# One launch with two transformer layers: score matmuls over 64 features, row differences and rotary partners by on-chip transfers, weights fetched one head group ahead

## The chip, the core and the metric

The kernel runs on one core of a Trainium2 chip. The core has five engines that matter here: TensorE (PE in the profile, with its weight loads as PEld), VectorE (DVE), ScalarE (ACT), GpSimd (POOL) and SyncE (SP), which issues nearly all transfers. Each engine runs its own instructions in the order in which they were written; between engines there are semaphores. The metric is the device time of one launch in microseconds, lower is better.

## What is computed

The input is `x`, 16 batches of 256 tokens with 256 features, and a second array of the same shape. Two layers follow, each of the form x = x + attention(condition(x)) and x = x + ffn(condition(x)). All numbers are fp32. The part that the change concerns is the second layer's attention:

```python
# condition: a reaction-diffusion step on the 256 x 256 array of one batch
lap_x = y[:, s, d-1] - 2 y[:, s, d] + y[:, s, d+1]      # reflected at the edges
lap_y = y[:, s-1, d] - 2 y[:, s, d] + y[:, s+1, d]      # reflected at the edges
u = zX * lap_x + zY * lap_y + zR * y * (1 - y)
# attention: 16 heads of 64 features, segments of 128 tokens, 16 memory keys and values per head
z = u * rsqrt(mean(u * u) + eps) * g
q, k, v = split(z @ W_qkv)
q, k = rotary(q), rotary(k)        # pairs of features (even, odd) are turned by an angle
scores = q @ concat(memory_k, k).T / 8     # inside a segment, causal
x = x + softmax(scores) @ concat(memory_v, v) @ W_out
```

Before it come a cross attention, a 16-head causal attention with 16 features a head and a feed-forward net on numbers quantized in blocks of 16. After it comes a mixture of experts: 8 experts, of which each token uses 2, and a shared one.

## The kernel before

**Two parts.** `woven` does everything up to the second attention, batch by batch; `mixture` does the rest. The change touches only `woven`, and `setup`, where an array in DRAM is made.

**Streams and the planner.** In `woven` each stage is a generator that yields single operations: `stage_a` and `stage_e` (cross attention and first attention), `stage_gate`, `stage_up`, `stage_down` (quantized weights, once), `stage_f` (first feed-forward net), `stage_p` (diffusion and projections), `stage_g` (scores and softmax), `stage_v` (values, output projection, store of the batch). `weave` keeps one waiting operation of each stream, estimates when it could start, and writes the earliest one next; ties go to the stream that stands earlier in the list. The estimate has a cost per operation, 0.15 us for a hop between engines (`HOP`), and 4.5 us from a transfer's issue until its data are there (`LANDING`). What it writes is a fixed order for every engine. Counters in `g.done` keep the stages apart: a group of four heads may be projected when fewer than three groups are ahead of the values; the diffusion of a batch begins when its feed-forward net is done.

**Diffusion** (`diffuse`). `y` is a batch as [128 partitions, 2, 256]: token s lies in partition s mod 128, half s div 128. The difference along the features is made by POOL from shifted slices. The difference along the tokens crosses partitions, and is a product with a constant 256 x 256 matrix `lap`: four matmuls into PSUM (`ply`), which DVE multiplies by `zy` and adds to `u`.

**Projection** (`project4`), for each of four groups of four heads, in each of 16 batches. The group's weights are loaded at its start: `wq` (two transfers), `wv`, `wo`. The columns of `w_qk1` come from the host ordered so that a 256-column block holds four heads' even features in its first 128 columns and the odd ones in the last. So PE leaves in `pq[:, 0, :]` the even features of four heads, 32 partitions each, and in `pq[:, 1, :]` the odd ones, for the same partitions. DVE multiplies by cosine into `f_t1` and by sine into `f_t2`; POOL makes two combinations of 128x256 each for the queries (`f_q`) and two for the keys (`keys0` to `keys3`, one tile per group, kept).

**Scores** (`scores4`). A head's 64 features lie in two pieces of 32 partitions. Each of two segments and four heads is therefore two matmuls of 32 rows by 144 columns that add up in PSUM: 16 a group, in two steps of two heads. DVE adds the mask and takes the maximum, ACT exponentiates, POOL scales.

**Order on the queues.** SP has the loads, the zero-writes of `ysort` (two of 1 MB a batch, in `stage_f`), the stores of a batch (`xd`) and all that the change adds. POOL has the joins, the first attention's triangular masks (`b_e`), the softmax scalings (`f_prob`, `f_pm`) and half of the quantization.

The names of the steps to follow: in `diffuse` (line 860) `lap`, `lx`, `u`; in `project4` (line 897) `wq`, `f_t1`, `f_t2`; in `scores4` (line 955) the innermost loop; in `project_heads` (line 467) `b_t1`, `b_t2`; in `weave` (line 182) the rule in `ready`.

Of the kernel before, what the change touches and what calls it, by code (L numbers as in the profile page):

```python
# [19 lines left out]
P = 128  # L20
S = 256
# [41 lines left out]
def setup(ctx, tc, a, n_batch):  # L63
# [28 lines left out]
    k.zero = c.tile([P, D], F32, name="zero")  # L92
    nc.gpsimd.memset(k.zero, 0.0)

    k.xd = [dram.tile([S, D], F32, name=f"xd{b}") for b in range(n_batch)]
# [86 lines left out]
def weave(streams):  # L182
# [8 lines left out]
    def ready(op, engine):  # L191
        t = 0.0
        for n in names(op.ins):
            when, by = written.get(n, (0.0, engine))
            t = max(t, when + (HOP if by != engine else 0.0))
        for x in op.outs:
            n = x.tensor.name
            before = [written.get(n), read.get(n)]
            ring = rings.get(getattr(x.tensor, "tag", None), [])
            if n not in ring and ring:  # L200
                bufs = x.tensor.bufs or x.tensor.tag_meta.bufs
                if len(ring) >= bufs:
                    before += [written.get(ring[-bufs]), read.get(ring[-bufs])]
            for p in before:
                if p:
                    t = max(t, p[0] + (HOP if p[1] != engine else 0.0))
        return t
# [84 lines left out]
def woven(k):  # L292
    nc, tc = k.nc, k.tc
    with ExitStack() as ctx:
# [12 lines left out]
        g.live, g.kT = {}, {}  # L307
        g.x, g.io, g.done = {}, {}, {"W": 0, "A": 0, "M": 0, "E": 0, "F": 0, "P": 0, "G": 0, "V": 0, "L": 0}
        with tc.manual_schedule():
            weave([stage_a(g), stage_e(g), stage_gate(g), stage_up(g), stage_down(g), stage_f(g), stage_p(g), stage_g(g), stage_v(g)])  # L310

# [101 lines left out]
def fetch_a(g, b):  # L413

    a = g.a
    g.x[b] = g.xp.tile([P, 2, D], F32, name="x", tag="x")
    xT = g.a_.tile([P, 2, S], F32, name="xT", tag="xT", bufs=2)
    fT = g.a_.tile([P, 2, S], F32, name="fT", tag="fT")
# [48 lines left out]
def project_heads(g, hT):  # L467
# [8 lines left out]
    for st in range(2):  # L476
# [11 lines left out]
        table = lambda t: t[:, st, :].unsqueeze(1).to_broadcast([P, 2 * H, DH0 // 2])  # L488
        t1, t2 = tile_a(g, 2 * D, "b_t1"), tile_a(g, 2 * D, "b_t2")
        for r in range(2):  # L490
            yield g.dve.tensor_tensor(pairs(t1)[:, :, :, r], pairs(qk)[:, :, :, r], table(g.cos0), ALU.mult)
            sin = table(g.sin0 if r else g.nsin0)
            yield g.dve.tensor_tensor(pairs(t2)[:, :, :, r], pairs(qk)[:, :, :, 1 - r], sin, ALU.mult)
        for i, dst in enumerate((qp, kp)):
            half = slice(i * D, (i + 1) * D)
            yield g.pool.tensor_tensor(dst[:, st, :, 0:DH0], by_head(t1[:, half]), by_head(t2[:, half]), ALU.add)

# [298 lines left out]


def stage_p(g):
    k, a = g.k, g.a
    yield lambda: g.done["A"] > 0 and g.done["W"] == 3  # L800
    g.lap, op = load(g, g.w, "lap", [P, 2, S], a["lap"])
    yield op
    g.z = []
# [34 lines left out]

    g.keys = []
    for n in range(4):  # L840
        pmk = tile_l(g, [P, 2, 4 * PM], "pmk", 2)
        yield g.sp.dma_start(out=pmk, in_=a["pmk"][:, n])
        t = g.w.tile([P, 2, 2, PM + P], F32, name=f"keys{n}")
        for j in range(4):
            rows = row32(j, 32)
            src = pmk[rows, :, j * PM : (j + 1) * PM]
            yield g.pool.tensor_copy(t[rows, :, :, 0:PM], src.unsqueeze(2).to_broadcast([32, 2, 2, PM]))
        g.keys.append(t)
    g.mhalf = g.w.tile([P, 2], F32, name="mhalf")
    yield g.pool.memset(g.mhalf, -0.5)  # L850
    for b in range(g.B):
# [44 lines left out]

def project4(g, n, zT):

    a = g.a
    wq = tile_l(g, [P, 2, 2, 2 * P], "wq", 2)  # L900
    for which in range(2):
        cols = slice((8 * which + 2 * n) * P, (8 * which + 2 * n + 2) * P)
        yield g.sp.dma_start(out=wq[:, which], in_=a["w_qk1"][:, :, cols])
    wv, wo = tile_l(g, [P, 2, 4 * DH1], "wv", 2), tile_l(g, [P, 2, D], "wo", 3)
    yield g.sp.dma_start(out=wv, in_=a["w_v1"][:, :, n * 4 * DH1 : (n + 1) * 4 * DH1])
    yield g.sp.dma_start(out=wo, in_=a["w_out1"][:, 2 * n : 2 * n + 2, :])
    q = tile_l(g, [P, 2, S], "f_q", 3)
    by_seg = lambda t: t.rearrange("p (s t) -> p s t", s=2)
    for which in range(2):
        one = yield from single(g, wq, zT)  # L910
        pq = one.rearrange("p (r t) -> p r t", r=2)
        for r in range(2):
            yield from mm_(g, pq[:, r, :], [(wq[:, which, c, r * P : (r + 1) * P], zT[:, c, :]) for c in range(2)])
        t1, t2 = tile_l(g, [P, 2, S], "f_t1"), tile_l(g, [P, 2, S], "f_t2")
        cos, sin = (g.cos1, g.sin1) if which else (g.cosq, g.sinq)
        yield g.dve.tensor_tensor(t1, pq, cos.unsqueeze(1).to_broadcast([P, 2, S]), ALU.mult)
        yield g.dve.tensor_tensor(t2, pq, sin.unsqueeze(1).to_broadcast([P, 2, S]), ALU.mult)
        g.singles.append(one)
        dst = [g.keys[n][:, r, :, PM:] if which else by_seg(q[:, r, :]) for r in range(2)]
        yield g.pool.tensor_tensor(dst[0], by_seg(t1[:, 0, :]), by_seg(t2[:, 1, :]), ALU.subtract)  # L920
        yield g.pool.tensor_tensor(dst[1], by_seg(t1[:, 1, :]), by_seg(t2[:, 0, :]), ALU.add)
    v = tile_l(g, [P, 2, 4 * DH1], "f_v", 3)
# [5 lines left out]
    g.singles.append(one)  # L928
    return q, v, wo

# [23 lines left out]

def scores4(g, n, q, v, wo):

    keys = g.keys[n]
    prob = tile_l(g, [P, 2, 4, PM + P], "f_prob", 2)
    if n % 2 == 0:
# [550 lines left out]
```

## Time and profile before

| what | value |
|---|---|
| median of three runs | 2944.68 us (2943.74 to 2948.99) |
| profiled execution: its own time | 2943.53 us |
| profiled execution: span | 2941.8 us |
| mean granted TensorE clock | 0.963 |
| last matmul of `woven` ends | about 1896 us |
| DMA over the span | 265.66 MB, mean 90 GB/s |
| POOL: joins of `f_q` and of `keys` | 128 + 128, mean 734 and 762 ns |
| DVE: product with the `lap` result | 16, mean 751 ns |
| SP: one 128 KB or contiguous 256 KB load | about 0.33 to 0.47 us of issue |

A busy time is the time in which at least one instruction of that engine ran. A group row gives line, engine, operation, the tile written and those read, the shapes, the number of records, then busy time and mean duration of one, then the engine's idle time just before them and what ended it. Nearly all operations of the woven part pass through one helper and have its line, L160; they are told apart by tile names. Records of an fp32 matmul come in pairs.

### The profile page before, as it was taken

To read this page: it belongs to the slowest core of one execution; us is meant where nothing else is said; L and a number is where in the kernel's file an instruction comes from. 1 tells how busy PE (TensorE), PEld (TensorE's weight loads), DVE (VectorE), ACT (ScalarE), POOL (GpSimd) and SP (SyncE) were. 2 spreads that over 40 slices of the span, in tenths; PEclk is the share of its full clock that TensorE was granted. 3 is DMA by queue.
4 is the path that set the end of the run, shared out by engine and by line. 5 is a ranking of instruction groups with operands and counts; after the bars stand their busy time and mean duration, and the time that the engine had idled before them with its cause. 6 is when DMAs were issued, how large, how long until landed. Compare 5 with 4: busy or idle time off the path is not lost. (4 is left out here: it accounts for less than half of the span.)

```text
span 2941.8 us, 42036 instructions
## 1 busy us (share of the span) xinstructions
PE 2768.7 (94%) x15979; PEld 2072.5 (70%) x15979; DVE 1428.6 (49%) x3073; ACT 924.0 (31%) x2416; POOL 842.2 (29%) x1023
## 2 busy tenths in 40 slices
PE   5899999999999999999999989689999999999999
PEld 3666667777777777767777767545566888888865
DVE  6566666676676676675776655413240000000023
ACT  2223333333333333423334333223321222222221
POOL 4333333433344343343343333202220000000034
PEclk7799999999899999999999999889999999999999
DMA  3122122122122132222221222231111355555523
GB/s 107 55 93 73 53 92 84 56 80 74 59 91 69 58 97 69 63 92 69 64 92 35 76 90 74 87 93 51 51 38 67 108 179 179 179 181 179 177 85 95
DMA packets 191230, 265.66 MB, mean 90 GB/s; under 512 B 34217, under 2 KB 161970, under 8 KB 181682
## 3 DMA queue, kind: packets, MB, share of 16 engines
q1 hardware_dynamic: 184882, 246.16, 26.2%
q0 software_dynamic: 6144, 16.79, 1.8%
q8 instruction: 128, 2.10, 0.3%
q14 instruction: 76, 0.62, 0.1%
HBM read 202.34 MB, written 60.56 MB: 89 GB/s over the span
## 5 line engine op out<-in xcount | busy, mean ns | idle before, releaser
L160 ACT ACTIVATE f_prob<-pair,f_stat 128x144 f32<-128x144 f32 x512 | 190.7, 377 | 270.2 <-DVE f_stat L160 258.8
L160 DVE TENSOR_TENSOR pair<-pair,mask 128x256 f32<-128x256 f32 (+1 forms) x384 | 197.8, 516 | 123.1 <-PE pair L160 83.2
L49 PE MATMUL bank<-ysT,w 128*128 128x256 f32 x1120 | 249.3, 381 | 5.7 <-ACT ysT L113 5.7
L160 PE MATMUL single<-e_zT,wq 128*128 128x256 f32 x1024 | 254.1, 392 | 0.0
L1155 POOL DMA_INDIRECT got<-osort,pos_o x64 | 62.3, 973 | 662.8 <-ACT hT L1103 608.5
L49 PE MATMUL bank<-w,ehT 128*128 128x256 f32 x1120 | 247.4, 379 | 0.0
L49 PEld LDWEIGHTS bank<-ysT,w 128*128 128x128 f32 x1120 | 211.3, 190 | 38.0 <-ACT ysT L113 9.9
L49 PEld LDWEIGHTS bank<-w,ehT 128*128 128x128 f32 x1120 | 212.8, 190 | 28.9
L160 PEld LDWEIGHTS single<-e_zT,wq 128*128 128x128 f32 x1024 | 193.4, 196 | 32.9 <-issue 2.7
L1140 ACT ACTIVATE ehT<-bank,own_b 128x256 f32<-128x256 f32 x280 | 132.5, 473 | 241.6 <-PE bank L49 241.6
L160 POOL TENSOR_SCALAR_AFFINE_SELECT b_e<-b_e 128x512 f32<-128x512 f32 x128 | 86.5, 676 | 329.9 <-ACT b_e L160 329.9
L160 PE MATMUL pair<-keys,f_q 32*128 32x144 f32 x2048 | 164.9, 300 | 0.9 <-ACT b_e L160 0.7
L160 PEld LDWEIGHTS pair<-keys,f_q 32*128 32x128 f32 x2048 | 137.2, 190 | 35.9 <-issue 28.6
L160 ACT ACTIVATE b_e<-pair 128x768 f32<-128x768 f32 x128 | 103.6, 810 | 166.4 <-PE pair L160 153.3
L160 PE MATMUL single<-wo,f_oT 128*128 128x256 f32 x512 | 129.8, 386 | 9.5 <-ACT f_oT L160 8.4
L160 POOL TENSOR_TENSOR f_q<-f_t,f_t 128x256 f32<-128x256 f32 x128 | 91.6, 734 | 160.9 <-DVE f_t L160 151.4
L160 PE MATMUL pair<-b_qkT 16*128 16x128 f32 (+1 forms) x1024 | 127.3, 373 | 11.0 <-ACT b_qkT L160 8.0
L1145 DVE COPY eo<-bank 128x512 f32<-128x512 f32 x35 | 24.2, 692 | 230.9 <-PE bank L49 230.9
L160 DVE TENSOR_REDUCE qpad<-pair 128x2 f32<-128x256 f32 (+1 forms) x256 | 131.0, 554 | 4.4
L1259 POOL DMA_INDIRECT ysort<-r_y,r_posi x64 | 62.6, 978 | 241.0 <-DMA ysort<-r_y,r_posi 97.0
L160 DVE TENSOR_TENSOR x<-x,single 128x512 f32<-128x512 f32 (+1 forms) x112 | 68.0, 607 | 128.7 <-PE single L160 128.1
L160 POOL TENSOR_TENSOR keys<-f_t,f_t 128x256 f32<-128x256 f32 x128 | 95.2, 762 | 118.8 <-DVE f_t L160 117.6
(295 smaller groups left out, 5319.7 us busy)
## 6 DMA issues: line engine op xcount, KB each, us to landing
w<-in_w SPq DMA_DIRECT2D x70, 1024.0 KB
ysort<-zero SPq DMA_DIRECT2D x32, 1024.0 KB
wq<-in_w_qk SPq DMA_DIRECT2D x128, 256.0 KB
wv<-in_w_v SPq DMA_DIRECT2D x64, 256.0 KB
wo<-in_w_out SPq DMA_DIRECT2D x64, 256.0 KB
ys<-ysort SPq DMA_DIRECT2D x35, 256.0 KB
osort<-eo SPq DMA_DIRECT2D x35, 256.0 KB
xT<-in_xT SPq DMA_DIRECT2D x16, 256.0 KB
```

The lines of the kernel that those rows point to most:

```text
L49: nc.tensor.matmul(out, lhsT, rhs, start=start and i == 0, stop=stop and i == last)
L160: return Op([(self.name, self.cost(fn, outs, aps), lambda: call(*args, **kw))], outs, aps)
L1140: nc.scalar.activation(hT[:, f, :], ph, AF.Gelu_apprx_tanh, bias=b1[:, f : f + 1])
L1145: nc.vector.tensor_copy(o, po)
L1155: nc.gpsimd.indirect_dma_start(out=g, out_offset=None, in_=k.osort[:, :], in_offset=bass.IndirectOffsetOnAxis(ap=r.pos_o[:, i, t : t + 1], ...
L1259: nc.gpsimd.indirect_dma_start(out=k.ysort[:, :], out_offset=bass.IndirectOffsetOnAxis(ap=posi[:, i, t : t + 1], axis=0), in_=y, in_offset ...
```

## The change

It has these parts.

- **Scores over 64 features.** The columns of the query and key weights are put in another order: for each pair of heads the 32 even and then the 32 odd features of one head, then of the other. A head then lies in 64 neighbouring partitions, and a score is one matmul of 64 rows. The reordering is done once on the chip, by a new stage `stage_order`, which loads eight blocks, has POOL copy them in the new order and stores them in a DRAM array `wqk`. `stage_p` waits for it.
- **Rotary partners by transfer.** Even and odd features of a head are now in different partitions. After DVE's products, four transfers of 32 partitions each exchange neighbouring blocks of the sine product from `f_t2` into `f_t3`, and POOL adds `f_t1` and `f_t3` in one 128x512 operation. The sign is in the sine table. The addition for the queries is written after the keys' transfers, that for the keys after the value projection.
- **Second difference by neighbours' rows.** The four `lap` matmuls go. `up` and `down` are `y` moved by one partition, each a transfer of 127 partitions, with four transfers of one partition for the rows at the edges of the halves. POOL adds them, DVE subtracts twice `y` and adds the product with `zy`.
- **Weights a group ahead.** `fetch_p` loads `wq` and `wv` for the next group before the present one is projected; `wo` is loaded in `scores4`.
- **Order of streams and the planner.** `stage_g` stands ahead of `stage_p` in the list, `stage_order` before `stage_f`. In `ready`, an operation of SP no longer waits for an earlier SP operation on the same buffer.
- **Space.** `xT` has one buffer instead of two; in `project_heads` the cosine product is written in place and `b_t1` goes; `f_t1` and `f_t3` have two buffers, `f_t2` one.

```diff
-            yield g.dve.tensor_tensor(pairs(t1)[:, :, :, r], pairs(qk)[:, :, :, r], table(g.cos0), ALU.mult)
             sin = table(g.sin0 if r else g.nsin0)
             yield g.dve.tensor_tensor(pairs(t2)[:, :, :, r], pairs(qk)[:, :, :, 1 - r], sin, ALU.mult)
+        for r in range(2):
+            yield g.dve.tensor_tensor(pairs(qk)[:, :, :, r], pairs(qk)[:, :, :, r], table(g.cos0), ALU.mult)
...
+def stage_order(g):
+
+    k = g.k
+    for i in range(8):
+        cols = slice(i * 2 * P, (i + 1) * 2 * P)
+        raw, out = tile_l(g, [P, 2, S], "f_t1", 2), tile_l(g, [P, 2, S], "f_t3", 2)
+        yield g.sp.dma_start(out=raw, in_=g.a["w_qk1"][:, :, cols])
+        for c in range(2):
+            dst = out[:, c].rearrange("p (j r d) -> p j r d", j=4, r=2)
+            yield g.pool.tensor_copy(dst, raw[:, c].rearrange("p (r j d) -> p j r d", r=2, j=4))
+        yield g.sp.dma_start(out=k.wqk[:, :, cols], in_=out)
+    g.done["O"] = 1
...
     for b in range(g.B):
-        yield lambda b=b: g.done["F"] > b
+        yield lambda: g.done["F"] > b
         zT = yield from diffuse(g, b)
         for n in range(4):
-            yield lambda i=4 * b + n: i < g.done["V"] + 3
-            g.live[4 * b + n] = yield from project4(g, n, zT)
-            g.done["P"] += 1
+            i = 4 * b + n
+            yield lambda: i < g.done["V"] + 3
+            ahead = (yield from fetch_p(g, (n + 1) % 4)) if i + 1 < 4 * g.B else None
+            g.live[i] = yield from project4(g, n, zT, *weights)
+            g.done["P"] = i + 1
+            weights = ahead
...
+def fetch_p(g, n):
+
+    wq = tile_l(g, [P, 2, 2, 2 * P], "wq", 2)
+    for which in range(2):
+        cols = slice((8 * which + 2 * n) * P, (8 * which + 2 * n + 2) * P)
+        yield g.sp.dma_start(out=wq[:, which], in_=g.k.wqk[:, :, cols])
+    wv = tile_l(g, [P, 2, 4 * DH1], "wv", 2)
+    yield g.sp.dma_start(out=wv, in_=g.a["w_v1"][:, :, n * 4 * DH1 : (n + 1) * 4 * DH1])
+    return wq, wv
...
 def diffuse(g, b):
...
-    one = yield from single(g, y)
-    ply = one.rearrange("p (s d) -> p s d", s=2)
-    for st in range(2):
-        yield from mm_(g, ply[:, st, :], [(g.lap[:, c, st * P : (st + 1) * P], y[:, c, :]) for c in range(2)])
+
+    up, down = tile_l(g, [P, 2, D], "e_up"), tile_l(g, [P, 2, S], "f_t3", 2)
+    for dst, src in (
+        (up[1:P], y[0 : P - 1]),
+        (down[0 : P - 1], y[1:P]),
+        (up[0:1, 1, :], y[P - 1 : P, 0, :]),
+        (down[P - 1 : P, 0, :], y[0:1, 1, :]),
+        (up[0:1, 0, :], y[1:2, 0, :]),
+        (down[P - 1 : P, 1, :], y[P - 2 : P - 1, 1, :]),
+    ):
+        yield g.sp.dma_start(out=dst, in_=src)
...
-    yield g.dve.scalar_tensor_tensor(u, ply, zy, u, ALU.mult, ALU.add)
-    g.singles.append(one)
+    yield g.pool.tensor_tensor(up, up, down, ALU.add)
+    yield g.dve.scalar_tensor_tensor(up, y, -2.0, up, ALU.mult, ALU.add)
+    yield g.dve.scalar_tensor_tensor(u, up, zy, u, ALU.mult, ALU.add)
...
-        t1, t2 = tile_l(g, [P, 2, S], "f_t1"), tile_l(g, [P, 2, S], "f_t2")
+        t1, t2, t3 = (tile_l(g, [P, 2, S], f"f_t{i}", 1 if i == 2 else 2) for i in (1, 2, 3))
...
-        dst = [g.keys[n][:, r, :, PM:] if which else by_seg(q[:, r, :]) for r in range(2)]
-        yield g.pool.tensor_tensor(dst[0], by_seg(t1[:, 0, :]), by_seg(t2[:, 1, :]), ALU.subtract)
-        yield g.pool.tensor_tensor(dst[1], by_seg(t1[:, 1, :]), by_seg(t2[:, 0, :]), ALU.add)
+
+        for i in range(4):
+            yield g.sp.dma_start(out=t3[row32(i, 32)], in_=t2[row32(i ^ 1, 32)])
+        dst = g.keys[n][:, :, :, PM:] if which else q.rearrange("p c (s t) -> p c s t", s=2)
+        yield from join
+        join = iter([g.pool.tensor_tensor(dst, by_seg(t1), by_seg(t3), ALU.add)])
...
         for st in range(2):
-            for r in range(2):
-                for i in range(2):
-                    rows = row32(j0 + i, 32)
-                    lhsT, rhs = q[rows, r, st * P : (st + 1) * P], keys[rows, r, st, :]
-                    yield g.pe.matmul(sc[i][:, st, :], lhsT, rhs, start=r == 0, stop=r == 1)
+            for i in range(2):
+                rows, c = row32(2 * i, 64), j0 // 2
+                lhsT, rhs = q[rows, c, st * P : (st + 1) * P], keys[rows, c, st, :]
+                yield g.pe.matmul(sc[i][:, st, :], lhsT, rhs, start=True, stop=True)
```

The memory keys are laid out to match, by eight small loads and one copy per group at the start.

More of the change, by code (lines that the diff above doesn't have):

```diff
@@ L93, in setup @@
     nc.gpsimd.memset(k.zero, 0.0)
+    k.wqk = dram.tile([P, 2, 2 * H * DH1], F32, name="wqk")
     k.xd = [dram.tile([S, D], F32, name=f"xd{b}") for b in range(n_batch)]
@@ L204, in ready @@
             for p in before:
-                if p:
+                if p and not p[1] == engine == "SP":
                     t = max(t, p[0] + (HOP if p[1] != engine else 0.0))
@@ L307, in woven @@
         g.live, g.kT = {}, {}
-        g.x, g.io, g.done = {}, {}, {"W": 0, "A": 0, "M": 0, "E": 0, "F": 0, "P": 0, "G": 0, "V": 0, "L": 0}
+        g.x, g.io, g.done = {}, {}, {"W": 0, "O": 0, "A": 0, "M": 0, "E": 0, "F": 0, "P": 0, "G": 0, "V": 0, "L": 0}
         with tc.manual_schedule():
-            weave([stage_a(g), stage_e(g), stage_gate(g), stage_up(g), stage_down(g), stage_f(g), stage_p(g), stage_g(g), stage_v(g)])
+            weave([stage_a(g), stage_e(g), stage_gate(g), stage_up(g), stage_down(g), stage_order(g), stage_f(g), stage_g(g), stage_p(g), stage_v(g)])
 def load(g, pool, name, shape, src):
@@ L416, in fetch_a @@
     g.x[b] = g.xp.tile([P, 2, D], F32, name="x", tag="x")
-    xT = g.a_.tile([P, 2, S], F32, name="xT", tag="xT", bufs=2)
+    xT = g.a_.tile([P, 2, S], F32, name="xT", tag="xT")
     fT = g.a_.tile([P, 2, S], F32, name="fT", tag="fT")
@@ L488, in project_heads @@
         table = lambda t: t[:, st, :].unsqueeze(1).to_broadcast([P, 2 * H, DH0 // 2])
-        t1, t2 = tile_a(g, 2 * D, "b_t1"), tile_a(g, 2 * D, "b_t2")
+        t2 = tile_a(g, 2 * D, "b_t2")
         for r in range(2):
-            yield g.dve.tensor_tensor(pairs(t1)[:, :, :, r], pairs(qk)[:, :, :, r], table(g.cos0), ALU.mult)
             sin = table(g.sin0 if r else g.nsin0)
             yield g.dve.tensor_tensor(pairs(t2)[:, :, :, r], pairs(qk)[:, :, :, 1 - r], sin, ALU.mult)
+        for r in range(2):
+            yield g.dve.tensor_tensor(pairs(qk)[:, :, :, r], pairs(qk)[:, :, :, r], table(g.cos0), ALU.mult)
         for i, dst in enumerate((qp, kp)):
             half = slice(i * D, (i + 1) * D)
-            yield g.pool.tensor_tensor(dst[:, st, :, 0:DH0], by_head(t1[:, half]), by_head(t2[:, half]), ALU.add)
+            yield g.pool.tensor_tensor(dst[:, st, :, 0:DH0], by_head(qk[:, half]), by_head(t2[:, half]), ALU.add)
 def row32(j, n):
@@ L795, in tile_l @@
     return g.l_.tile(shape, F32, name=name, tag=tag or name, bufs=bufs)
+def stage_order(g):
[9 more added lines that the diff above has]
+    g.done["O"] = 1
 def stage_p(g):
     k, a = g.k, g.a
-    yield lambda: g.done["A"] > 0 and g.done["W"] == 3
-    g.lap, op = load(g, g.w, "lap", [P, 2, S], a["lap"])
-    yield op
+    yield lambda: g.done["A"] > 0 and g.done["W"] == 3 and g.done["O"]
     g.z = []
@@ L839, in stage_p @@
     g.keys = []
+    pmk = tile_l(g, [P, 4, 2, PM], "pmk")
+    for j in range(4):
+        for r in range(2):
+            src = a["pmk"][row32(j, 32), :, r, j * PM : (j + 1) * PM]
+            yield g.sp.dma_start(out=pmk[row32(2 * (j % 2) + r, 32), :, j // 2, :], in_=src)
     for n in range(4):
-        pmk = tile_l(g, [P, 2, 4 * PM], "pmk", 2)
-        yield g.sp.dma_start(out=pmk, in_=a["pmk"][:, n])
         t = g.w.tile([P, 2, 2, PM + P], F32, name=f"keys{n}")
[L844 to L847, printed above, removed]
+        yield g.pool.tensor_copy(t[:, :, :, 0:PM], pmk[:, n].unsqueeze(2).to_broadcast([P, 2, 2, PM]))
         g.keys.append(t)
+    for rows in (row32(1, 32), row32(3, 32)):
+        for t in (g.sin1, g.sinq):
+            yield g.pool.tensor_scalar(t[rows], t[rows], -1.0, None, ALU.mult)
     g.mhalf = g.w.tile([P, 2], F32, name="mhalf")
     yield g.pool.memset(g.mhalf, -0.5)
+    weights = yield from fetch_p(g, 0)
     for b in range(g.B):
-        yield lambda b=b: g.done["F"] > b
+        yield lambda: g.done["F"] > b
         zT = yield from diffuse(g, b)
         for n in range(4):
-            yield lambda i=4 * b + n: i < g.done["V"] + 3
-            g.live[4 * b + n] = yield from project4(g, n, zT)
-            g.done["P"] += 1
+            i = 4 * b + n
[12 more added lines that the diff above has]
+    return wq, wv
 def diffuse(g, b):
@@ L894, in diffuse, with project4 @@
     return zT
[L897 to L906, printed above, removed]
+def project4(g, n, zT, wq, wv):
     q = tile_l(g, [P, 2, S], "f_q", 3)
-    by_seg = lambda t: t.rearrange("p (s t) -> p s t", s=2)
+    by_seg = lambda t: t.rearrange("p c (s t) -> p c s t", s=2)
+    join = ()
     for which in range(2):
@@ L928, in project4 @@
     g.singles.append(one)
-    return q, v, wo
+    yield from join
+    return q, v
 def stage_g(g):
@@ L952, in stage_v, with scores4 @@
             g.done["L"] = b + 1
-def scores4(g, n, q, v, wo):
+def scores4(g, n, q, v):
     keys = g.keys[n]
+    wo = tile_l(g, [P, 2, D], "wo", 2)
+    yield g.sp.dma_start(out=wo, in_=g.a["w_out1"][:, 2 * n : 2 * n + 2, :])
     prob = tile_l(g, [P, 2, 4, PM + P], "f_prob", 2)
```

## The prediction

> **What bounds the kernel now.** The page's busy rows come first, then busy time by stretch.
>
> ```profile
> span 2941.8 us, 42036 instructions
> PE 2768.7 (94%) x15979; PEld 2072.5 (70%) x15979; DVE 1428.6 (49%) x3073; ACT 924.0 (31%) x2416; POOL 842.2 (29%) x1023
> ```
>
> ```profile
> 100.00:300.00 200.00, 181.72 (x1090) 129.22 (x1088) 126.02 (x254) 60.37 (x139) 74.34 (x103) 0.92 0.22 71
> 600.00:1600.00 1000.00, 958.28 (x6571) 726.43 (x6570) 688.06 (x1378) 359.00 (x1058) 386.26 (x459) 0.97 0.24 74
> 1700.00:1896.00 196.00, 172.87 (x1162) 139.42 (x1160) 107.41 (x211) 65.13 (x246) 67.15 (x81) 0.92 0.22 69
> ```
>
> The columns of a stretch are its length, the busy time of PE, PEld, DVE, ACT and POOL, then granted clock, DMA share and GB/s. The woven part, which is all that the change touches, ends at about 1896 us. In its middle PE idles 42 of 1000 us, so each microsecond of PE work taken out there is worth nearly one. At the head PE idles 18 of 200 us, at the tail 23 of 196; less work returns less there. The chain of waits shows only the last 130 us, in the mixture, which stays as it is. The other engines have room: DVE 69%, POOL 39% in the middle.
>
> Next the groups with shapes kept apart (busy, mean ns), and matmuls in order of time:
>
> ```profile
> L160 PE MATMUL single<-e_zT,wq 128*128 128x256 f32 x1024 | 254.1, 392 | 0.0
> L160 PE MATMUL pair<-keys,f_q 32*128 32x144 f32 x2048 | 164.9, 300 | 0.9 <-ACT b_e L160 0.7 <-DVE vpad L160 0.2
> L160 PE MATMUL single<-x,lap 128*128 128x256 f32 x128 | 31.3, 387 | 0.0
> ```
>
> ```profile
> 1017.22 1.25 PE L160 MATMUL pair<-keys,f_q 32*128 32x144 f32 x16
> ...
> 1018.67 1.89 PE L160 MATMUL single<-e_zT,wq 128*128 128x256 f32 x8
> ...
> 1021.35 1.09 PE L160 MATMUL single<-ident,f_prob 128*128 128x128 f32 x8
> ```
>
> An fp32 matmul leaves two records. A 256-column record over the full array takes 1.89/8 = 236 ns, a 128-column one 136 ns; 144 columns lie between, about 148 ns. The score records take 1.25/16 = 78 ns: two run at a time.
>
> **What goes from PE.** Scores: 16 records of 32 rows become 8 of 64 rows, at each of 128 places. The next work began 1.18 us after a score block, so the blocks occupy 128 x 1.18 = 151 us. No row shows 64-row pairs. If two overlap as now, 75 us go; if they ran alone, 8 x 148 ns = 1.18 us, nothing would. [...] 78 ns against 148 is two-fold. I take the row: 75 us. The 64-column value matmuls of the same trace (16 records in 1.09 us, 68 ns each) show half-array tiles overlapping two-fold. The `lap` matmuls go too: 128 x about 0.23 = 29 us. Together **104 us**.
>
> **What is hidden.** DVE gains one 128x512 operation of about 0.75 us a batch, 12 us in all, at 69% busy. POOL exchanges 256 joins of 734 and 762 ns for 128 of about 1.28 us (its 128x512 row), 191 us for 164, and gets one 1.28 us addition a batch. Of the weights a group ahead I expect nothing: no matmul on `wq` waited before. `xT` with one buffer costs nothing, as its reader is done before the next load; `b_qk` written in place makes DVE wait for POOL once a batch, at most the 1.7 us of the two additions, beside other matmuls.
>
> **SP's queue** goes from 451 to 1078 planned transfers in the woven part. The instruction order shows that each waits for the eighth before it. A heads' shuffle is 4 transfers of 32 rows, some 0.37 us of SP each (a one-piece `wo` load took 0.34), 1.5 us, and the first small load of the trace landed 1.8 us after its issue ended:
>
> ```profile
> 0.82 1.87 SPq L78 DMA_DIRECT2D idx<-in_itok_B  x3
> ```
>
> ```profile
> 4.53 0.38 DVE L81 CAST idxf<-idx 64x48 f32<-64x48 int32 x1 [4.53 <-DMA idx<-in_itok_B]
> ```
>
> (4.53 - 2.69.) With two DVE products before (1.36) and the join behind (1.28) that is 6 to 8 us. In the changed order the matmuls between the projection and the first that must wait for its shuffle are worth 10 to 24 us in batches 5 to 12: hidden. In the last 24 shuffles they are worth 4 to 12: about 0.6 us each, **15 us**. The new `stage_order` puts 16 transfers of 256 KB and 16 POOL copies (0.85 us each by the 128x256 `cosq` row, 14 us) among the first weights, where PE idles anyway; SP's order makes later loads wait for those copies: 0 to 20, I take **8 us**.
>
> **The neighbours' rows decide.** `up` and `down` are moves of 127 partitions, 260 KB each, and POOL's sum waits for both. Behind it in POOL's order stand the masks `b_e`, the softmax scalings and the next joins; DVE's next product waits for the sum, and behind that stand maxima, masks and copies, which PE needs. The queue row gives one engine's rate:
>
> ```profile
> q1 hardware_dynamic: 184882, 246.16, 26.2%
> ```
>
> 246.16 MB in 26.2% of 16 x 2941.8 us is 20 GB/s for each of 16 engines; in the busiest stretch it is 184/(16 x 0.55) = 21. By that row alone, spread over 16 engines, a move takes 0.8 us. [...] Then a move takes 260/21 = 12.4 us, both share that engine, and the pair takes 25 us. No transfer before has such a size, so the trace cannot confirm it[...].
>
> The way around it: copy, product and shuffle issue ahead of the moves, and their own issue, 3.8 us; data 24.9; landing 1.8; then the sum 1.3, the product 0.7 and the rest up to the first waiting matmul about 4. Sum 36.5 us. Against it stands the PE work in between, counted in the changed order and priced by the trace: in batches 5 to 12 always 114 matmuls, 20 of 256 columns (0.47 us), 8 of 352 (0.66), 26 transposes and the like (0.27), 28 `b_qkT` at 0.22, 32 narrower ones, together 31 us. In batches 0 to 4 it is 7, 23, 26, 17 and 23 us; in 13 to 15, 16, 13 and 14.
> - Middle: 8 x (36.5 - 31.3) = 42 us.
> - First five: 29 + 13 + 11 + 19 + 13 = 85 us; last three: 20 + 24 + 22 = 66 us. At both ends PE idled already (41 us in the two stretches above); such waits now lie inside the new ones. I take off 45: 106 us.
>
> **Sum** against the profiled execution's own 2943.5 us (the median of the runs is 2944.7): 2943.5 - 104 + 148 + 15 + 8 = 3010; a little of the head's loss may hide behind the weights' stage, so **3005 us**.
>
> **Rivals.**
> - **Faster, the moves are short or covered.** Spread over 16 engines they land in 4 us, and everything is covered: 2943.5 - 104 + 15 + 8 = 2862; with part of the cover lost, to 2900. For it: the 31 us of cover in eight batches; at 25 GB/s (the quickest stretches of packets are better than the mean) the middle's loss is near zero. Against it: [...] short covers at the ends.
> - **Even.** One engine, but 10.4 us a move: the way is 32.5, the loss 10 + 119 - 45 = 84, and 2943.5 - 104 + 84 + 23 = 2947. For it: an idle machine's engine is quicker than the mean of a shared one.
> - **Much slower, no gain in the scores.** If pairs of 64 rows do not overlap, 75 us come back: 3080. Against it: the value matmuls' 68 ns. A worse way ends there too: if the single engine also delays the shuffles and weight loads queued behind (SP stops at the eighth), the middle loses 15 us a batch.
> - That the change doesn't do what it says: the order shows 512 score matmuls for 1024 and no `lap`; this is out.
>
> **Chances.** Likeliest case 0.62, faster 0.26, even 0.06, much slower 0.06. The likeliest alone spans 2955 to 3065. The range takes in the short moves and most of the lost overlap: 2865 to 3085. A change below 0.2% (6 us) can't be told from none here: faster 0.26, same 0.06, slower 0.68.
>
> **What would show it.** `keys,f_q` at about half its busy time with 1024 records, `lap` gone: the gain. POOL idle before `e_up` with a DMA as releaser, 16 times, and PE waits of 5 us in the middle and 10 to 25 us at the ends: the loss. A DMA share near 1/16 during those waits shows the single engine. If POOL's wait for `e_up` is a few us, [...] the time is near 2865. If PE waits for `keys` and `f_q` in the middle, the shuffles were priced too low. If score records double to 150 ns, the overlap was wrong.

## The result, and the profile after

The changed kernel takes 3109.76 us (median of 4 runs, 3102.15 to 3120.67) against 2944.25 us for the kernel before on the same chip: 1.0563 times as long, 95% interval 1.0537 to 1.0589. The forecast was 3005, with a range of 2865 to 3085. The direction was right, and so was the cause of the loss; the gain that was set against it mostly did not come, and the forecast is too low by 105 us.

The head of the page of the changed kernel, then the woven part in one stretch (from PE's first transpose of `b_o` to the last matmul of `woven`) for the kernel before and for the changed one. Columns: stretch, length, busy PE, PEld, DVE, ACT, POOL, granted clock, DMA share, GB/s.

```profile
span 3100.4 us, 41071 instructions
...
PE 2734.2 (88%) x14827; PEld 2010.6 (65%) x14827; DVE 1452.7 (47%) x3073; ACT 933.4 (30%) x2432; POOL 855.2 (28%) x919
```

```profile
94.98:1896.00 1801.02, 1697.00 (x11458) 1282.22 (x11456) 1194.64 (x2389) 633.95 (x1884) 674.42 (x819) 0.96 0.23 72
```

```profile
99.73:2054.01 1954.28, 1659.57 (x10306) 1218.48 (x10304) 1216.86 (x2389) 642.28 (x1900) 680.33 (x699) 0.91 0.30 88
```

The span grew by 158.6 us. The woven part starts 4.7 us later and is 153.3 us longer: PE's busy time fell by 37.4, its idle time rose from 104.0 to 294.7. The mixture behind it is unchanged. By batch, from the starts of those transposes: batches 0 to 5 took 673.5 us for 595.3, the eight in the middle 903.3 for 887.0, the last two with the drain 377.5 for 318.7.

The idle time is the neighbours' rows. These are POOL's and DVE's waits over the whole span (total, times, longest):

```profile
POOL e_up L161 <- DMA f_t<-x: 190.4, 16, 26.7
DVE e_up L161 <- POOL e_up L161: 173.9, 16, 25.9
```

Sixteen waits, one a batch, and DVE waits behind POOL. One of them, in a steady batch, as SP's queue and then POOL's timeline show it (start, duration, idle before), with the DMA share while the moves are under way:

```profile
1052.67 0.71 SPq L161 DMA_DIRECT2D e_up<-x  x1
1053.56 4.18 SPq L161 DMA_DIRECT2D f_t<-x  x1
1057.79 9.92 SPq L161 DMA_DIRECT2D e_up<-x  x1
```

```profile
1077.01 1.26 POOL L161 TENSOR_TENSOR e_up<-e_up,f_t 128x512 f32<-128x512 f32 x1 [3.28 <-DMA f_t<-x]
```

```profile
1062.00:1074.00 12.00, 10.22 (x77) 6.75 (x78) 11.65 (x18) 5.66 (x15) 9.84 (x10) 0.86 0.07 26
```

From the issue of `up` to POOL's sum pass 24.3 us. `down` takes 4.18 us of SP to issue, and the one-row move after it 9.92 us, where the other one-row moves take 0.58 to 0.59. Behind the short moves of e1 below, the same one-row move takes 0.56 us in one steady batch; so the long moves hold up the queue, by what means no run shows. PE then meets the delay as one large wait in each of the first five batches. Its waits in the stretch 99 to 773 us:

```profile
PE single L161 <- POOL f_prob L161: 24.0, 1, 24.0
PE single L161 <- ACT c_xT L161: 21.9, 1, 21.9
PE single L161 <- DVE a_e L161: 18.2, 2, 17.9
PE single L161 <- DVE b_o L161: 14.9, 4, 13.6
PE single L161 <- POOL b_e L161: 14.8, 2, 14.7
```

The named releasers differ, but each stands behind `e_up` in POOL's or DVE's order, or is fed from there: all five waits end 1.9 to 4.0 us after POOL begins the sum. In the middle stretch the same thing is 18.8 us in eight waits (for `a_e`), in the last three batches 61.8 (`e_u` 37.1 in three waits, `f_pT` 24.7 in one).

The gain that was to pay for this, in the groups of PE (busy, mean ns):

```profile
L161 PE MATMUL single<-e_zT,wq 128*128 128x256 f32 x1024 | 267.7, 408 | 1.8 <-ACT e_zT L161 1.7
L161 PE MATMUL pair<-keys,f_q 64*128 64x144 f32 x1024 | 101.9, 318 | 12.9 <-POOL keys L161 12.7
```

The scores fell from 164.9 to 101.9 us and the 31.3 us of `lap` are gone: 94.3 us less. But the `wq` matmuls, whose number and shape stay, rose from 254.1 to 267.7, and other groups rose too; only 37.4 of the 94.3 remain. The next fence shows one reason: four stretches around the large wait at 487 us, and PE's timeline there and around a short wait in a steady batch.

```profile
470.00:485.00 15.00, 14.62 (x109) 10.87 (x110) 10.14 (x25) 7.67 (x24) 6.62 (x8) 1.00 0.47 157
485.00:500.00 15.00, 2.14 (x28) 1.33 (x24) 0.31 (x1) 1.50 (x5) 0.10 (x1) 0.68 0.23 74
500.00:505.00 5.00, 2.77 (x15) 1.67 (x16) 3.65 (x7) 1.31 (x7) 2.08 (x3) 0.50 0.01 3
505.00:510.00 5.00, 4.65 (x21) 3.66 (x21) 2.62 (x8) 2.69 (x10) 1.53 (x3) 0.77 0.00 0
```

```profile
501.80 1.50 PE L161 MATMUL single<-b_e,vpad 128*32 128x256 f32 x12 [14.65 <-POOL b_e L161]
503.73 3.76 PE L161 MATMUL single<-wo,f_oT 128*128 128x256 f32 x8 [0.43 <-DVE f_oT L161]
...
508.99 1.89 PE L161 MATMUL single<-e_zT,wq 128*128 128x256 f32 x8
...
1152.44 1.12 PE L161 MATMUL single<-ident,d_h 128*128 128x128 f32 x4 [2.22 <-POOL d_h L161]
1153.35 3.14 PE L161 MATMUL single<-e_zT,wq 128*128 128x256 f32 x8
```

The granted clock goes from 1.00 to 0.50 and comes back about 6 us after PE works again. Eight `wo` records take 3.76 us there; the eight `wq` records of the same shape at 508.99 take 1.89. This stall of 14.65 us is thus paid twice: once as idle, once as slow work. A shorter wait is enough in this trace: after 2.22 us without work the eight `wq` records at 1153.35 take 3.14 us, and the granted clock of 1150:1155 is 0.75.

How much of the lost gain is the clock can be bounded. The clock records of both traces hold only 1.00 and 0.50, and PE's busy time at 0.50 in the woven part is 130.5 us before and 199.6 after. At that rate the eight records above take 3.76 us for 1.89, so the rate can have added at most half of that time, and explains, as an estimate, at most 35 of the 57 us. (The mean of 0.91 says less: of the 338 us at 0.50, PE idles in 138.) What added the other 22 or more was not found.

### The profile page after: what moved, and what is told of

Its sections match the earlier page's. It is cut to its first block, busy times and chain, and to the rows that moved or that the text cites. A ratio compares the mean times of both kernels' runs of the same rounds, so it can differ in the third digit from the quotient of the medians.

```text
span 3100.4 us, 41071 instructions
## 1 busy us (share of the span) xinstructions
PE 2734.2 (88%) x14827; PEld 2010.6 (65%) x14827; DVE 1452.7 (47%) x3073; ACT 933.4 (30%) x2432; POOL 855.2 (28%) x919
## 5 line engine op out<-in xcount | busy, mean ns | idle before, releaser
L161 PE MATMUL single<-e_zT,wq 128*128 128x256 f32 x1024 | 267.7, 408 | 1.8 <-ACT e_zT L161 1.7
L161 PEld LDWEIGHTS single<-e_zT,wq 128*128 128x128 f32 x1024 | 201.0, 205 | 38.0 <-ACT e_zT L161 3.6
L161 PE MATMUL single<-wo,f_oT 128*128 128x256 f32 x512 | 138.8, 406 | 12.0 <-ACT f_oT L161 9.3
L161 POOL TENSOR_TENSOR f_q<-f_t,f_t 128x512 f32<-128x512 f32 x64 | 81.3, 1271 | 190.1 <-DMA f_t<-f_t 170.8
L161 PE MATMUL pair<-b_qS,b_qkT 17*128 17x256 f32 (+1 forms) x1024 | 122.1, 360 | 10.6 <-DVE qpad L161 7.3
L161 PE MATMUL single<-wv,e_zT 128*128 128x256 f32 x512 | 125.9, 389 | 0.0
L161 POOL TENSOR_TENSOR f_prob<-f_prob,f_stat 128x1024 f32<-128x1024 f32 x64 | 125.4, 1960 | 0.0
L161 PEld LDWEIGHTS pair<-b_qS,b_qkT 17*128 17x128 f32 x1024 | 96.6, 198 | 43.3 <-DVE qpad L161 9.5
```

Source lines behind the costliest of these rows:

```text
L161: return Op([(self.name, self.cost(fn, outs, aps), lambda: call(*args, **kw))], outs, aps)
```

## Experiments

All kernels start from the changed kernel or from one named. Beside each median stands its ratio to the kernel before with the 95% interval. "Woven" is the stretch defined above, in each kernel's own trace. The last four columns are those of one profiled execution, which lies up to 14 us off the median (e3 13.7 and e6 11.1 above, e15 12.7 below).

| kernel | median us | ratio to before | woven us | PE busy | PE idle | clock |
|---|---|---|---|---|---|---|
| before | 2944.25 | 1 | 1801.0 | 1697.0 | 104.0 | 0.96 |
| changed | 3109.76 | 1.0563 (1.0537 to 1.0589) | 1954.3 | 1659.6 | 294.7 | 0.91 |
| e1 moves cut at 112 rows | 2932.93 | 0.9968 (0.9948 to 0.9988) | 1779.0 | 1631.1 | 147.9 | 0.95 |
| e4 moves cut at 113 rows | 3067.69 | 1.0423 (1.0399 to 1.0447) | 1917.1 | 1656.2 | 260.9 | 0.92 |
| e3 planner told 25 us | 3111.93 | 1.056 (1.0532 to 1.0589) | 1978.0 | 1682.9 | 295.0 | 0.90 |
| e2 lap matmuls kept | 2945.31 | 1.0005 (0.9991 to 1.002) | 1790.5 | 1651.6 | 138.8 | 0.97 |
| e7 before + moves at 112 | 2953.67 | 1.0042 (1.0029 to 1.0054) | 1808.2 | 1664.7 | 143.5 | 0.95 |
| e5 e1, rank undone | 3017.3 | 1.0267 (1.0225 to 1.031) | 1873.8 | 1674.4 | 199.4 | 0.94 |
| e10 before + rank | 2933.82 | 0.9974 (0.9962 to 0.9986) | 1790.3 | 1691.5 | 98.8 | 0.97 |
| e8 e1, order by host | 2935.04 | 0.9984 (0.997 to 0.9998) | 1785.5 | 1634.3 | 151.2 | 0.95 |
| e6 e1, price mended | 2917.94 | 0.9917 (0.9889 to 0.9946) | 1781.0 | 1636.9 | 144.1 | 0.95 |
| e9 e6 + e8 | 2914.56 | 0.9919 (0.9897 to 0.9941) | 1766.3 | 1633.3 | 132.9 | 0.95 |
| e11 e2, price mended | 2918.67 | 0.9928 (0.9905 to 0.995) | 1774.9 | 1637.1 | 137.8 | 0.97 |
| e13 e11, order by host | 2915.84 | 0.9915 (0.9887 to 0.9943) | 1767.4 | 1633.9 | 133.5 | 0.97 |
| e14 changed, price mended | 3160.86 | 1.0752 (1.0718 to 1.0785) | 2012.0 | 1657.5 | 354.5 | 0.90 |
| e12 e9, SP's issue priced | 3126.42 | 1.0622 (1.0591 to 1.0653) | 1988.7 | 1747.2 | 241.5 | 0.90 |
| e15 e13, no shuffles | 2881.8 | 0.9807 (0.9774 to 0.984) | 1726.6 | 1625.6 | 101.0 | 0.97 |
| **e16 e13, two f_t2** | **2868.94** | 0.9756 (0.9725 to 0.9787) | 1725.9 | 1625.4 | 100.5 | 0.97 |
| e17 e9, two f_t2 | 2936.13 | 0.9978 (0.9966 to 0.9989) | 1793.2 | 1645.4 | 147.9 | 0.94 |
| e18 e2, two f_t2 | 2921.7 | 0.9932 (0.9906 to 0.9958) | 1773.8 | 1646.2 | 127.7 | 0.96 |

### The moves of 127 rows

**e1: each move cut into one of 112 rows and one of 15.**

```diff
-        (up[1:P], y[0 : P - 1]),
-        (down[0 : P - 1], y[1:P]),
+        (up[1:113], y[0:112]),
+        (up[113:P], y[112 : P - 1]),
+        (down[0:112], y[1:113]),
+        (down[112 : P - 1], y[113:P]),
```

> Each move of 127 partitions is cut into one of 112 and one of 15; nothing else is changed. Theory [...]: the 24.3 us from the first move's issue to POOL's sum fall to 6 to 9 us, the 182 us of PE waits behind the sum go nearly whole, the granted clock of the woven part returns to 0.95 or more, and the time is 2880 to 2920 us, below the kernel before. Rival (the queue is crowded by the 512 shuffles and SP's eight places, and the moves only suffer with it): two more transfers a batch, the sum waits as long, 3100 us or more.

Measured: 2932.93 us, 177 less than the changed kernel, though it moves the same bytes and issues two moves more per batch. The row of the 112-row moves in eight steady batches (KB each, median us from issue to landing), and POOL's waits over the whole span:

```profile
e_up<-x SPq DMA_DIRECT2D x8, 224.0 KB, 2.7
```

```profile
POOL e_up L161 <- DMA f_t<-x: 19.2, 5, 7.3
```

2.7 us from issue to landing in place of some 24 to the sum, and 19.2 us of POOL's waits in place of 190.4. As an estimate, 224 KB in 2.7 us are 85 GB/s, over three times the 26 GB/s at a DMA share of 0.07 with the long moves under way, so more than one engine carries such a piece. How long the moves take is what costs. The time is above the 2880 to 2920 expected; that is taken up below.

**e4: the same cut one row further on**, 113 and 14 rows. It tells the row count from the mere number of pieces.

> As the cut into 112 and 15, but into 113 and 14[...]. Theory [...]: the large piece stays on one engine, the way from issue to POOL's sum is 113/127 of before plus little, 21 to 23 us, and the time is 3080 to 3110 us. Rival (any cut helps[...]): near the cut into 112 and 15.

Measured: 3067.69 us, 135 more than with 112 rows. SP's queue and POOL's sum in one batch:

```profile
1040.28 3.48 SPq L161 DMA_DIRECT2D e_up<-x  x2
1043.88 8.84 SPq L161 DMA_DIRECT2D f_t<-x  x2
```

```profile
1062.64 1.28 POOL L161 TENSOR_TENSOR e_up<-e_up,f_t 128x512 f32<-128x512 f32 x1 [1.32 <-DMA f_t<-x]
```

22.4 us from issue to sum, as expected, and the issue again blocks SP. With e1 this shows that the row count decides, not the number of pieces; what sets 112 apart from 113 and 127 was not shown. The total is 12 us better than its bracket.

**e3: the planner told the truth about these moves**, so that it may write other work before the sum.

```diff
         end = start + cost + (LANDING if engine == "SP" else 0.0)
+        if engine == "SP" and op.outs[0].shape[0] == P - 1:
+            end = start + 25.0
```

> Only the planner's estimate is changed: a transfer of 127 partitions counts as landed 25 us after its issue, instead of 4.5. The moves themselves stay. Theory (the loss is a wait that the written order does not foresee, and other batches' work could fill it): the waits of 14 to 24 us in the first five and last three batches shrink to half, 3000 to 3050 us; the last three stay long because no other batch's work is left. Rival (the transfer's length itself sets the pace): 3090 to 3120 us.

Measured: 3111.93 us, nothing gained. POOL waits 186.9 us for the moves, where the changed kernel had 190.4. Knowing the delay does not help the planner; that the streams offer it too little work to put in front is a likely reason that was not tried.

### What the other parts of the change gave

**e2: the lap matmuls kept**, everything else changed.

```diff
-    up, down = tile_l(g, [P, 2, D], "e_up"), tile_l(g, [P, 2, S], "f_t3", 2)
...
-        yield g.sp.dma_start(out=dst, in_=src)
+    one = yield from single(g, y)
+    ply = one.rearrange("p (s d) -> p s d", s=2)
...
+    yield g.dve.scalar_tensor_tensor(u, ply, zy, u, ALU.mult, ALU.add)
```

> The second difference goes back to the four matmuls with lap; the scores over 64 features, the shuffles, the weights ahead and the stream order stay as changed. Theory (all of the loss is in the moves): PE work is 63 us below the kernel before, shuffle waits of some 10 to 25 us at the end and 5 us at the start come on top, 2895 to 2925 us. Rival (shuffles and stream order cost too): 2945 us or more.

Measured: 2945.31 us, as the rival said. PE is busy 45.4 us less than before, and idle 34.8 more. The 10.6 us between them do not show in the median, as the profiled execution took 2937.55. So without the moves the rest of the change is worth nothing, and the moves as written cost the whole loss (164 us above e2). And the scores' gain of 63 us is spent elsewhere: PE is some 18 us busier here than their removal leaves, at a granted clock no lower than before, and 34.8 us go into idle.

**e7: the moves alone**, at 112 rows, on the kernel before (the second difference of e1 in place of `lap`).

```diff
-xT = g.a_.tile([P, 2, S], F32, name="xT", tag="xT", bufs=2)
+xT = g.a_.tile([P, 2, S], F32, name="xT", tag="xT")
...
-    one = yield from single(g, y)
...
+    up, down = tile_l(g, [P, 2, D], "e_up"), tile_l(g, [P, 2, S], "e_down")
```

> The kernel before with only the second difference changed: neighbours' rows by moves cut at 112 rows in place of the four lap matmuls per batch (and one xT buffer in place of two, for room). Theory: the PE sets the pace, so its 31.3 us of lap go from the time, less some 5 to 10 for the longer way to u: 2915-2925 us. Rival: PE time that is freed turns into waits for POOL and DVE, as in the kernel where the scores alone were changed: 2932-2948 us.

Measured: 2953.67 us, 0.4% slower than before. 32.3 us of PE's busy time are gone and 39.5 us of idle have come. Even short moves are no gain here.

**e5 and e10: the rank of scores over projections**, undone in e1 and done alone in the kernel before.

```diff
-stage_f(g), stage_g(g), stage_p(g), stage_v(g)
+stage_f(g), stage_p(g), stage_g(g), stage_v(g)
```

> The cut at 112 rows (2932.9 us) with the projections ranked over the scores again, as before the change. Theory: the rank is part of what eats the gain of the scores, because the planner lets the scores take the PE first and the queries and keys of the next group then come late by way of the on-chip transfers: 2900-2925 us, and the PE's waits for POOL's keys (13.3 us of the cut kernel) shrink below 7. Rival: the rank helps or does nothing, because the chain of waits is set by softmax and POOL's product f_prob: 2928-2970 us, keys not shrunk.

> The kernel before with the scores ranked over the projections and nothing else. Theory: the rank is worth something only where the projections end in an on-chip transfer, so that here it moves little: 2935-2960 us. Rival: the rank by itself is the gain that the rank undone cost in the cut kernel (84 us) in part: below 2925 us. Second rival: it costs the kernel before, and the change as a whole had to carry that: above 2970 us.

Measured: 3017.3 us without it (84 more than e1), 2933.82 with it alone (9 less than before, between the cases named). In e5 PE's waits for `keys` did shrink (13.3 to 5.9 us over the whole span), as the theory had it, and those for DVE's `qpad` grew from 15.4 to 37.1; the theory falls. The rank is a small gain by itself and worth 84 us in e1; which other part of the change needs it was not separated.

**e8: the new column order made before the launch.** `stage_order` goes, `fetch_p` reads `w_qk1`.

```diff
-...reshape(D, 2, 4, 4, DH1 // 2, 2).transpose(0, 1, 2, 5, 3, 4)
+...reshape(D, 2, 4, 4, DH1 // 2, 2).transpose(0, 1, 2, 3, 5, 4)
```

> The cut at 112 rows, with the columns of w_qk1 laid out in the new order before the launch, so that the stage that reorders them (16 POOL copies, 16 moves) is gone. Theory: only the start gets its 4.7 us back: first work on b_o at 95-96 us in place of 100.5, 2926-2930 us. Rival: the weights come from another region or the planner's order shifts by chance: anything from 2918 to 2940 with the first b_o unmoved or the periods changed.

Measured: the first `b_o` starts at 94.7 in place of 100.5 us, but the median, 2935.04, does not tell from e1's. Five microseconds saved at the start were lost in the order that followed.

### The planner's price for a score

The planner lets two matmuls run beside each other when they have 32 rows or fewer. For the new 64-row matmuls it therefore counts 4 x 0.288 = 1.15 us a block, as for the old ones (8 x 0.149), where the trace shows 0.76, with the next work 0.69 after its start. The order was written for a PE that is slower than the real one.

```diff
-            side = (2 if rows <= 32 else 1) * (3 if cols <= 32 else 2 if cols <= 64 else 1)
+            side = (2 if rows <= 64 else 1) * (3 if cols <= 32 else 2 if cols <= 64 else 1)
```

**e6 (on e1), e11 (on e2), e9 (e6 with e8's column order), e14 (on the changed kernel).**

> The cut at 112 rows with one thing told to the planner: two matmuls of 64 rows run beside one another as two of 32 rows did, so a block of scores costs 0.6 us in its model and not 1.15 (0.76 measured). Theory: the written order rests on the wrong price, PE comes to its next work earlier than the order was written for, and the other engines are late: 2915-2927 us, idle of the PE in 100:1890 below 145 us (158.7 in the cut kernel). Rival: the order is insensitive to one price: 2928-2940 us.

> Scores of 64 rows with the lap matmuls kept (2945.3 us) and the planner's price for the scores mended. Theory: the wrong price is why the 63 us of the scores did not appear; 2915-2930 us, the waits of the PE in 100:1900 below 130 us (149). Rival: the gain of the price belongs to the kernel with the moves alone: 2938-2952 us.

> The cut at 112 rows with the planner's price for the scores mended (2917.9 us) and the new column order laid out before the launch (2935.0 alone). Theory: the two add up to the price's gain alone, since the start's 5 us go again in the order that follows: 2912-2922 us. Rival: an order written anew falls by chance, and the price's 15 us were chance too: 2925-2945 us.

> The changed kernel with its moves of 127 rows left as they are and only the planner's price for the scores mended. Theory: the moves' 24 us set the early and late batches and fill the steady ones, so that the price has nothing to gain there: 3095-3115 us. Rival: price and moves add up: 3080-3095 us.

Measured: 15 us less in e6, 27 less in e11, and e9 keeps it (2914.56). The times fell where the theory had them. The idle times did not: e6 idles 152.8 us in 100:1890, where below 145 was expected, and e11's woven part 137.8, where e2 has 138.8 (the theory wanted less than 130 for 149, over 100:1900, which in e11 takes in the start of the mixture). e6's trace is of its slowest execution, 2929.06 us, so it says little of a gain in the median; in e11's the gain is busy time, 1637.1 for 1651.6. So the price is worth the time, but not by the way the theory gave.

e14 went against both of its theories: 51 us slower than the changed kernel. POOL's waits for the moves:

```profile
POOL e_up L161 <- DMA f_t<-x: 265.8, 15, 27.5
```

They grew from 190.4, and PE's idle by 60 us. A likely reason, not tested: the packed order leaves less work in front of a sum that the planner believes to be 4.5 us away.

**e12: SP's issue priced at 0.5 us in place of 0.06**, on e9.

```diff
         if self.name == "SP":
-            return 0.06
+            return 0.5
```

> As the kernel with price and column order mended, and the planner told that SP needs 0.5 us to issue a move in place of 0.06 (the four moves of a shuffle took 2.5 to 2.7 us to issue in the cut kernel's trace). Theory: the order then knows when SP is late, and POOL's waits for the shuffles (217 us in the cut kernel) and the PE's for keys shrink: 2890-2912 us. Rival: SP is not late enough anywhere to set the pace: 2912-2930 us, as without it, or worse by chance.

Measured: 3126.42 us, a plain miss of both brackets. The steady period went from about 107 to 126 us, in its woven part PE waits 52.9 us for `f_prob` and 49.6 for `c_y`. A price nearer to what the trace shows gave a much worse order; why was not found.

### The single buffer behind the shuffles

The four moves of a shuffle read `f_t2`, which has one buffer, so DVE cannot write the next sine product until they have landed. **e13** is e11 with e8's column order, and the base of what follows.

> Scores of 64 rows with the lap matmuls kept, the planner's price mended (2918.7 us so far) and the column order laid out before the launch. Theory: the start's 5 us come on top: 2908-2918 us. Rival: the order written anew takes them back: 2918-2930 us.

Measured: 2915.84 us, within the theory, though not clearly below e11. Among DVE's waits in its woven part:

```profile
DVE f_t L160 <- DMA f_t<-f_t: 48.7, 29, 2.7
```

29 times DVE stands still for a shuffle, 48.7 us in all. From e13 start **e16**, with two buffers, and **e15**, which leaves the exchange out and adds `f_t2` in its own rows, so that it no longer computes the rotation (it has two buffers of `f_t2` too). The "first kernel" of both texts is e13.

```diff
-        t1, t2, t3 = (tile_l(g, [P, 2, S], f"f_t{i}", 1 if i == 2 else 2) for i in (1, 2, 3))
+        t1, t2, t3 = (tile_l(g, [P, 2, S], f"f_t{i}", 2) for i in (1, 2, 3))
```

```diff
-        for i in range(4):
-            yield g.sp.dma_start(out=t3[row32(i, 32)], in_=t2[row32(i ^ 1, 32)])
...
-        join = iter([g.pool.tensor_tensor(dst, by_seg(t1), by_seg(t3), ALU.add)])
+        join = iter([g.pool.tensor_tensor(dst, by_seg(t1), by_seg(t2), ALU.add)])
```

> As the first kernel of this call, but with the four on-chip moves per projection left out: the sine's products are added in their own rows in place of their neighbours', which leaves the exchange out of the rotation. Theory: the shuffles (4.3 us from product to sum, 217 us of POOL's waits in the cut kernel) are what keeps the scores' 63 us from showing beyond the 24 seen: 2875-2895 us. Rival: they are hidden, and the PE's freed time is lost to the other waits: within 8 us of the first kernel of this call.

> As the first kernel of this call, with two buffers for f_t2, which each shuffle's moves read, in place of one. Theory: DVE no longer waits for the moves of the projection before (38.6 us in the changed kernel), but DVE is not the bound: within 8 us of the first kernel. Rival: DVE's wait held up qpad and x, which the PE waits for: 8 to 20 us less.

Measured: 2881.8 without shuffles, 34 less than e13; 2868.94 with shuffles and two buffers, 47 less, more than either theory said. In e16 DVE waits for no shuffle any more, while POOL waits no less for them: 202.9 us in the two rows below, where e13 has 195.0. With two buffers in both, the kernel without shuffles is no faster than the one with them (their profiled executions took 2869.10 and 2869.26 us). So the way through the transfers is hidden on this base, and what cost was the single buffer. POOL's waits, the woven part and `wq` in e16:

```profile
POOL f_q L160 <- DMA f_t<-f_t: 159.0, 41, 8.6
POOL keys L160 <- DMA f_t<-f_t: 43.9, 24, 5.3
```

```profile
94.60:1820.54 1725.94, 1625.43 (x10434) 1213.34 (x10432) 1202.29 (x2366) 631.00 (x1907) 643.47 (x683) 0.97 0.32 95
```

```profile
L160 PE MATMUL single<-e_zT,wq 128*128 128x256 f32 x1024 | 254.7, 392 | 1.9 <-ACT e_zT L160 1.9
```

PE is busy 71.6 us less than before and idles as long (100.5 for 104.0), and `wq` has its old 392 ns. Here the scores' gain is in the time: 2868.94 us, 2.4% below the kernel before and 241 us below the changed one.

**e17 and e18: the second buffer elsewhere**, with the moves at 112 rows (on e9), and with the old price and `stage_order` (on e2).

> Neighbours' rows by moves cut at 112 rows, price and column order mended (2914.6 us so far), and two buffers for f_t2. Theory: DVE's wait for the single f_t2 was the common brake, and with it gone the lap's 31 us of PE time show too, beyond the kernel that keeps the lap matmuls (2868.9): 2840-2858 us. Rival: the moves' longer way to u costs what the lap saves, as in the kernel before with the moves alone (ratio 1.0042): 2862-2885 us.

> Scores of 64 rows with the lap matmuls kept, old price and reordering stage as in the change (2945.3 us), and two buffers for f_t2 alone. Theory: the single buffer alone held the scores' gain back, the price only moved around it: 2868-2885 us. Rival: both are needed, and the buffer gives here some 20 us: 2918-2930 us.

Measured: e18 gains 24 us (2921.7), the rival's figure: neither the buffer alone nor the price alone (e11) frees the gain. e17 is 2936.13, 22 us slower than without the buffer, worse than both brackets. With two `f_t2`, moves in place of matmuls cost 67 us (e17 against e16). Why was not found; PE waits 15.1 us for `e_u` there, and e9 shows no such wait among its larger ones.

**What stays open.** Each edit makes the planner write a new order for all engines, and e8, e12, e14 and e17 show that an order can take back what an edit gives, or more. The 135 to 177 us of the moves are far outside that. The 47 us of the buffer go with a wait of the same size that vanished, but the same edit gives 24 us in e18 and takes 22 in e17, so how much of the 47 is order stays open. The 15 to 27 of the price are of the size of such shifts, and were not isolated with a fixed order. Nor was it isolated why the moves at 112 rows gain so little beside the `lap` matmuls: 12 us (e1 against e2), nothing at the mended price (e6 against e11, e9 against e13), and losses in e7 and e17.

## Why the prediction was right in direction and wrong in size

The step that failed is "each microsecond of PE work taken out there is worth nearly one": 94.3 us of work went, and PE is 37.4 us less busy. The second is the 45 us taken off the waits. The sum said +67 us on the profiled execution's span, and +158.6 came. The 91 us between them are the terms below. (The other 13 or so of the 105 between the forecast and the median: 5 taken off the sum at its end, and 7.6 by which the median lies above the profiled execution, which took 3102.15 us.)

- **PE's gain: the failed term.** 104 us were put in, 37.4 came, an error of 67. The score groups gave 63.0 and not 75: a block of eight records takes 0.76 us and the next work starts 0.69 us after the block's start, so the pairs of 64 rows do overlap, about 1.7-fold (0.69 us for eight is 86 ns each, against the 148 ns estimated for one alone), but the forecast halved the old block's 1.18 us to 0.59, and 0.69 came. `lap` gave 31.3 for 29. The rest, about 57 us, came back as busy time; the rows of the other groups, added up over the span, are 49 us longer. At most 35 of the 57 are the clock, by the estimate above: the prediction had no term for what a stall does to the work after it. The other 22 or more have no cause shown, and e2 has some 18 us of the kind without a lower clock. e16, which idles as little as before, has `wq` at 392 ns again and keeps the gain.
- **The waits.** 193 us gross were forecast for the moves (42 in the middle, 85 early, 66 late); 172.7 can be read off (18.8, 92.1, 61.8). The early and late ones are good to 10%. In the middle the loss was half the forecast: in the batch shown the sum came 24.3 us after the issue of `up`, where data and landing alone were put at 27. The 45 us taken off because PE idled at both ends before were the mistake: without the large waits 122 us of idle remain, more than the 104 of before. Here the old idle was not absorbed by the new waits. With the 15 us put in for the shuffles, idle was forecast at +163 and came at +191: an error of 28.
- **One DMA engine for 127 rows: right.** No trace of the kernel before shows it: the 25 us for the pair were the author's estimate, 260 KB at the 21 GB/s of one engine for each move, on the assumption that one engine carries both. With the moves under way the DMA share is 0.07 (1062:1074 us), about one engine in 16, at 26 GB/s; e1 with 2.7 us for 112 rows and e4 with 22.4 us to the sum for 113 fit it.
- **Start:** 4.7 us for 8. POOL's copies there take 0.40 us, not 0.85.
- **The shuffles:** their moves take 0.59 us of SP each, not 0.37, and POOL waits for them, hidden as forecast. Missed was DVE behind the single `f_t2` (38.6 us of waits in the changed kernel): the prediction weighed the in-place `b_qk` and the one `xT`, and not the buffer that a transfer now reads.
- **The rivals.** The even case (10.4 us a move) had the move nearer to the truth than the likeliest one, and its sum was too low all the same, by the two terms above. An engine quicker than the mean of 20 GB/s is there in the kernel before: its stretch 2220:2240 us has 65 GB/s at a DMA share of 0.16, which is 25 GB/s for one of 16. The order of SP in which a transfer waits for the eighth before it can be read in both traces: after the first eight, each transfer of SP signals on the semaphore of the eighth before it, 670 of 670 before and 1297 of 1297 in the changed kernel. The short moves' 2862 to 2900 was not reached by e1, where the moves are short: 2932.9. That branch carried 0.26 of the chance on a gain of PE time that the planner's order did not deliver.

## What to carry to other kernels

Count PE time taken out as time gained only if every producer that feeds PE can follow, and look for the one-buffer tile that a new transfer reads: one more buffer was worth 47 us in one kernel here and 24 in another, though it cost 22 in a third. Before moving rows between partitions, look at the row count: 127 cut into 112 and 15 saved 177 us here. Where a planner writes the order, look at the price of a changed operation too (mended, it gave 15 and 27 us here, and took 51 beside the long moves). And an added stall of TensorE was paid twice here, as idle and as slow work after it (191 us of idle and up to 35, as an estimate, of slow work): charge it so.

## What the runs showed of the hardware that was not expected

- After a stall of 14.65 us TensorE's granted clock was 0.50 in 500:505 us, where its work set in, and 0.77 in 505:510; eight 256-column records took 3.76 us for 1.89. A wait of 2.22 us was followed by the half rate too (3.14 us for eight such records).
- Long moves block the issuing queue: behind two moves of 127 rows SP needed 9.92 us to issue a move of one row, which takes 0.58 otherwise, and nothing else of SP's list went out meanwhile.
- One row decides: a move of 112 rows lands 2.7 us after issue, the pairs of 113 + 14 need 22.4 us from issue to sum, and the kernels differ by 135 us.
